# An LSTM on one core: VectorE's PSUM reads put ahead of the x sums, the cell over 128 columns, outer sums deferred

## The chip, the cores and the metric

The kernel runs on one core of one Trainium2 chip. Five engines of that core work side by side, each with its own queue that it takes strictly in order: TensorE (PE in the profile, its weight loads PEld), VectorE (DVE), ScalarE (ACT), GpSimd (POOL) and SyncE (SP), which here issues nearly all DMAs. [...] The metric is the time of one launch in microseconds (us), the median of several runs.

## The reference

An LSTM over 512 time steps, batch 32, input and state width 512, then a residual:

```python
xW = jnp.einsum('ntd,dg->ntg', x, Wx) + b          # x: 32 x 512 x 512, Wx: 512 x 2048
def step(carry, xw_t):
    prev_h, prev_c = carry
    a = xw_t + prev_h @ Wh                         # Wh: 512 x 2048
    i, f, o = sigmoid(a[:, :512]), sigmoid(a[:, 512:1024]), sigmoid(a[:, 1024:1536])
    g = jnp.tanh(a[:, 1536:])
    next_c = f * prev_c + i * g
    next_h = o * jnp.tanh(next_c)
out = x + hs                                       # hs: all next_h, h0 = cond_1024, c0 = 0
```

All of it is float32. `prev_h @ Wh` is a chain over the steps; `x @ Wx` depends on no step and can be made at any time before it is needed.

## The kernel before

**Layout.** A gate matrix of one time step (32 x 2048) is kept as 128 partitions (4 blocks of units x 32 batch rows) by 512 columns: two halves of 256, each four gates of 64 units. Two PSUM tiles `gates` take turns, one per step.

**The recurrence.** In step `k`, `h_part(k)` (L452) adds `h @ Wh` to `gates[k % 2]`, which `seed_gates` (ScalarE, L437) has filled with the step's x part from the SBUF tile `xw`. Then `cell(k)` runs: sigmoid, tanh, sigmoid on ScalarE (L482 to L484); on VectorE `f*c` (L486, 128 columns), and then by halves of 64 columns `i*g` (L491), `c` (L493), on ScalarE `tanh c` (L495), on VectorE `o*tanh c` (L498, written into the buffer called `fc`) and a transpose to `ht` (L507). `h_part(k+1)` reads `ht`. GpSimd adds `ht` to the residual x (L513, tile `oc`) and, for a later step, the bias to `xw` (L418).

**The x part.** `x @ Wx` is made in the gaps of the recurrence. Rows of 8 time steps go three at a time through a scheme of fast matrix multiplication with 20 products instead of 24 (lists `A_OPS`, `A_OF`, `B_OF`, `C_OPS`, `C_OF`), and each product through an inner scheme with 7 small products instead of 8. A superblock is 24 time steps (3 rows) and 20 products, which are called jobs. Windows are the slots for this work; from step 3 on there is one per step (`windows_of(k) = [k + 4]`). In a superblock's 24 windows the jobs start in five of every six (`begin`). One job spreads over six windows: in the window `v` of its start and the four behind it PE makes its small products 1, 5, 6, 7, 2, 3 and 4 (`products`, L273). Before them:

- x sums (VectorE): `node_sums` (L236) adds whole rows where the outer scheme wants it (128 x 512), and `inner_sums` (L203 to L206) makes the four 128 x 128 sums of a job. Both operands lie in SBUF. All are made in `prepare(v + 1)`, at the end of the window before the job's.
- `evacuate(v)` takes results out of PSUM: first `job.finish(half)` for the jobs that started five and four windows ago, which makes the outer sums (L380, VectorE, 128 x 512 a half, one operand in PSUM or both in SBUF; L371 is a plain ScalarE copy into a slot), and, with the second half, stores finished ones to DRAM (SP, L323). Then ScalarE copies `pu`, `p5`, `pp` (L297, L301, L307, L308) and VectorE adds `pu` (L304) and `pp` (L309), which read the PSUM tiles `acc`.

PE's first small product of a window is written into an `acc` tile, so it comes behind the VectorE and ScalarE reads of that tile.

**What sets the order.** The program is written in one order by hand (`tc.manual_schedule()`); each engine takes its own instructions in that order. Per step of the loop: `load_residual` and `load_xw(k+3)` (SP), `h_part(k)`, `seed_gates(k+1)`, `add_bias(k+2)`, then for the window `evacuate(v)`, `products(v)`, `fetch(v)` (SP: the factors `wa`, `wb` and, three windows ahead of a superblock, its three rows of x), `cell(k)`, and `prepare(v+1)`. So VectorE's queue between two cells reads: x sums of the next job, outer sums, `pu`, `pp`. While VectorE is in it, PE makes `h_part` and then the small products.

Jobs begin at step 10 (`START`, `LEAD = 22`): the steps before make three rows by another scheme and the 14 combined factors (`make_factors`). After the last job, from step 495 on, the gates are split in two halves of 64 units which overlap (`is_split`).

Of the kernel before, what the change touches and what calls it, by code (L numbers as in the profile page):

```python
# [1 line left out]

# [38 lines left out]
LEAD = 22  # L41
# [23 lines left out]
def kernel(  # L65
# [13 lines left out]
    npool = ctx.enter_context(tc.tile_pool(name="npool", bufs=7))  # L79
    spool = ctx.enter_context(tc.tile_pool(name="spool", bufs=6))  # L80
# [117 lines left out]
    def inner_sums(a, name):  # L198
# [3 lines left out]
        return s, [  # L202
# [13 lines left out]
    nodes = {}  # L216
# [7 lines left out]
    def node_sums(sb, n):  # L224

        ops = []

        def want(v):
            if v < 2 * MO or (sb, v) in nodes:
                return  # L230
            how, a, b = A_OPS[v - 2 * MO]
            want(a)
            want(b)
            dst = nodes[sb, v] = npool.tile([P, ROW, 2, B], F32, name=f"n_{sb}_{v}", tag="node")
            fn = nc.vector.tensor_add if how == "add" else nc.vector.tensor_sub
            ops.append(lambda: fn(dst, node(sb, a), node(sb, b)))  # L236

        want(A_OF[n])
        return ops

    def left(a, s, sums):
        if s in (1, 2, 4):
            return a(*{1: (0, 0), 2: (0, 1), 4: (1, 1)}[s])
        return sums[:, {5: 0, 6: 1, 7: 2, 3: 3}[s]]
# [37 lines left out]
    def products(v):  # L282
        for late, ss in ((1, (6,)), (4, (4,)), (2, (7,)), (0, (1,)), (0, (5,)), (1, (5,)), (3, (2, 3))):
            job = jobs.get(v - late)
            for s in ss if job else ():
                if s != 5 or job.w5 == v:
                    product(job, s)

    def evacuate(v):
        for half, late in ((1, 5), (0, 4)):  # L290
            job = jobs.get(v - late)
            if job:
                job.finish(half)
# [9 lines left out]
        if job:  # L303
            nc.vector.tensor_add(job.pu[:, 1], job.acc, job.p5)  # L304
        job = jobs.get(v - 3)
        if job:
            nc.scalar.copy(job.pp[0], job.pu)  # L307
            nc.scalar.copy(job.pp[1][:, 0], job.acc)  # L308
            nc.vector.tensor_add(job.pp[1][:, 1], job.acc, job.p5)  # L309

# [3 lines left out]
    spare = [const.tile([P, 2, 2 * C], F32, name=f"slot_{i}") for i in range(3)]  # L314
# [10 lines left out]
    def finish_unit(job, i, j):  # L325
        def finish(half):
# [3 lines left out]
            if half:  # L330
                store(i, j, job.f)
                free.append(job.f)

# [15 lines left out]
    for v in C_OF:  # L349
        uses[v] += 1  # L350
        if v < R:
            copied.add(v)
    sums, left_uses = {}, {}

    def finish_product(job, sb, n):
        def slot(v, half):
            if half == 0:
                sums[sb, v] = free.pop(0)
                left_uses[sb, v] = uses[v]
            return sums[sb, v][:, half]  # L360

        def done(v, half):
            if half and (sb, v) in left_uses:
                left_uses[sb, v] -= 1
                if left_uses[sb, v] == 0:
                    free.append(sums.pop((sb, v)))

        def finish(half):
            pp = job.pp[half].rearrange("p n c -> p (n c)")
            if n in copied:  # L370
                nc.scalar.copy(slot(n, half), pp)  # L371
# [3 lines left out]

            for v in by_ready[n]:
                how, a, b = C_OPS[v - R]
                fn = nc.vector.tensor_add if how == "add" else nc.vector.tensor_sub
                srcs = source(a), source(b)
                fn(slot(v, half), *srcs)  # L380
                for u in (a, b):
                    if u != n or n in copied:
                        done(u, half)
            for at, v in enumerate(C_OF):
                if ready[v] == n and half:
                    i, j = divmod(at, NJ)
                    store(HEAD // ROW + MO * sb + i, j, sums[sb, v])
                    done(v, half)
# [52 lines left out]
    HALVES = [slice(0, H), slice(H, P)]  # L441
# [23 lines left out]
    def cell(t):  # L465
# [9 lines left out]
        for part in [(0,), (1,)] if two else [(0, 1)]:  # L475
            units = slice(H * part[0], H * (part[-1] + 1))
            i = slice(part[0], part[-1] + 1)
            if two:
                g = half_of(t, part[0]).rearrange("p (h g u) -> p h g u", h=1, g=G)
            else:  # L480
                g = gates[t % 2].rearrange("p h (g u) -> p h g u", g=G)
            nc.scalar.activation(s[:, i, 0:2], g[:, :, 0:2], AF.Sigmoid)  # L482
# [210 lines left out]
```

## Time and profile before

| | |
|---|---|
| median of 3 runs (lowest, highest) | 3450.46 us (3447.96, 3450.6) |
| the profiled execution: its own time, its span | 3446.5 us, 3444.4 us |
| PE busy | 3170.1 us (92%) |
| VectorE busy | 2858.1 us (83%), 8502 instructions |
| ScalarE busy | 1529.9 us (44%) |
| GpSimd busy | 960.3 us (28%) |
| DMA | 649.90 MB, 189 GB/s on average |
| granted PE clock | 0.996 |

How to read the lines that follow. In a timeline each row has the start, the busy time, the engine, the line of the kernel, the operation, the tile written and those read with their shape, and how many instructions in a row it stands for; brackets at the end give how long the engine had been idle before and what released it. `x2` with 0.35 us means that two instructions of a group took that long together, since a second one starts before the first has ended. In a group row the two numbers behind the bar are the busy time in all (us) and the mean of one (ns), and behind the next bar idle time before it. In the view of waits a row has the total, the number and the longest, in us. In the view of stretches a row has the length and then, per engine, the busy time and the instructions in parentheses.

A step is counted from one L482 (the first sigmoid, which starts as soon as `h_part` has ended and ScalarE is free) to the next.

### The profile page before, as it was taken

Reading aid. Unit: us, or ns where it says so; the run is one execution under the profiler, and the core shown is the slowest. Engines: PE = TensorE matmul, PEld = TensorE weight load, DVE = VectorE, ACT = ScalarE, POOL = GpSimd, SP = SyncE. Lnnn points to the kernel's source line nnn. Section 1 sums busy time; section 2 is a strip of 40 time slices with the busy share of each in tenths; the row PEclk is TensorE's granted clock in tenths of the full one; section 3 lists DMA queues with packets and bytes.
Section 4 is the critical chain, followed back from the end, with each engine's and each line's share of the span. In section 5 each row is a group of like instructions: output and inputs, shape, how many; then the busy total and the mean of one; then the engine's idle time right before and its main releaser. Section 6 shows DMA issues by size and latency. Waiting matters only on the chain.

```text
span 3444.4 us, 103490 instructions
## 1 busy us (share of the span) xinstructions
PE 3170.1 (92%) x40948; PEld 1295.2 (38%) x40948; DVE 2858.1 (83%) x8502; ACT 1529.9 (44%) x4972; POOL 960.3 (28%) x1003
## 2 busy tenths in 40 slices
PE   8899999999999999999999999999999999999987
PEld 2433333333333333333333333333333333333334
DVE  5778888888888888988888888888888888888875
ACT  1344444444444444444444444444444444444433
POOL 0122322232222223222222222222223222232321
PEclk9999999999999999999999999999999999999999
DMA  4556665656666566656566565656565666666552
GB/s 179 168 192 211 187 211 177 209 175 198 190 190 215 169 212 195 202 168 215 173 203 190 189 209 178 211 185 210 167 216 170 205 190 187 208 184 214 173 154 66
DMA packets 324919, 649.90 MB, mean 189 GB/s; under 512 B 43600, under 2 KB 109264, under 8 KB 323920
## 3 DMA queue, kind: packets, MB, share of 16 engines
q1 hardware_dynamic: 324288, 643.28, 59.8%
q8 instruction: 320, 5.24, 0.7%
q14 instruction: 167, 1.37, 0.1%
q10 hardware_dynamic: 144, 0.01, 0.0%
HBM read 464.59 MB, written 178.52 MB: 187 GB/s over the span
## 4 chain that ended last, share of the span: by engine, by line
DVE 45%; PE 37%; ACT 6%; issue 6%; DMA 5%; POOL 1%; SPq 1%; DVEq 0%; POOLq 0%; ACTq 0%
PE gates L452 20%; PE acc L273 7%; DVE s L204 7%; PE pp L273 7%; DVE slot L380 4%; DVE n L236 4%; DMA row<-in_x_dram 4%; DVE s L203 3%; DVE pp L309 3%; DVE ht L507 3%; DVE s L205 3%; DVE raw L380 3%; DVE t L380 2%; DVE fc L498 2%; DVE ig L491 2%
## 5 line engine op out<-in xcount | busy, mean ns | idle before, releaser
L452 PE MATMUL gates<-wh_sb,ht 128*32 128x512 f32 (+1 forms) x16320 | 1820.0, 587 | 21.0 <-DVE fc L490 15.3
L513 POOL TENSOR_TENSOR oc<-xr,ht 128x128 f32<-128x128 f32 x495 | 304.2, 615 | 2406.6 <-DVE ht L507 1196.0
L452 PEld LDWEIGHTS gates<-wh_sb,ht 128*32 128x32 f32 x16320 | 521.6, 110 | 1033.0 <-issue 819.2
L418 POOL TENSOR_TENSOR xw<-xw,bias_sb 128x512 f32<-128x512 f32 x504 | 675.6, 1341 | 63.3 <-DMA xw<-xw 54.6
L482 ACT ACTIVATE s<-gates 128x256 f32<-128x256 f32 (+1 forms) x511 | 195.3, 382 | 695.0 <-PE gates L452 694.4
L307 ACT COPY pp<-pu 128x512 f32<-128x512 f32 x412 | 246.1, 597 | 368.6 <-DVE slot L380 166.8
L486 DVE TENSOR_TENSOR fc<-s,c 128x128 f32<-128x128 f32 x494 | 141.7, 287 | 271.6 <-ACT s L482 270.5
L495 ACT ACTIVATE ig<-c 128x64 f32<-128x64 f32 x1024 | 207.9, 248 | 288.8 <-DVE c L493 288.8
L273 PE MATMUL acc<-wa,s 128*32 128x256 f32 x2240 | 176.5, 387 | 160.3 <-DVE pp L309 157.7
L204 DVE TENSOR_TENSOR s<-s,n 128x128 f32<-128x128 f32 x280 | 288.4, 1030 | 9.7
L308 ACT COPY pp<-acc 128x256 f32<-128x256 f32 x412 | 146.9, 357 | 332.6 <-DVE slot L380 126.1
L437 ACT COPY gates<-xw 128x512 f32<-128x512 f32 x493 | 284.8, 578 | 20.0 <-DVE xw L410 19.7
L498 DVE TENSOR_TENSOR fc<-s,ig 128x64 f32<-128x64 f32 x1024 | 192.5, 226 | 103.4 <-ACT ig L495 103.4
L309 DVE TENSOR_TENSOR pp<-acc,p 128x256 f32<-128x256 f32 x412 | 175.5, 426 | 89.5 <-ACT pp L308 80.5
L273 PE MATMUL pp<-wb,n 128*32 128x256 f32 x3200 | 245.9, 379 | 0.0
L273 PEld LDWEIGHTS acc<-wa,s 128*32 128x32 f32 x2240 | 54.5, 108 | 382.9 <-DVE pp L309 322.4
L273 PE MATMUL acc<-wb,s 128*32 128x256 f32 x2240 | 172.6, 380 | 19.2 <-DVE pu L304 19.2
L491 DVE TENSOR_TENSOR ig<-s 128x64 f32<-128x64 f32 x1024 | 187.3, 223 | 0.0
L507 DVE STREAM_TRANSPOSE ht<-fc 128x64 f32<-128x64 f32 x990 | 184.1, 224 | 1.8 <-DVE fc L498 1.6
L493 DVE TENSOR_TENSOR c<-fc,ig 128x64 f32<-128x64 f32 x1024 | 182.9, 218 | 1.2
L297 ACT COPY pu<-acc 128x256 f32<-128x256 f32 x412 | 152.4, 370 | 50.7 <-PE acc L273 41.5
L273 PE MATMUL acc<-t,s 128*32 128x256 f32 x1920 | 146.3, 384 | 30.3 <-DVE pu L304 16.5
(140 smaller groups left out, 4290.1 us busy)
## 6 DMA issues: line engine op xcount, KB each, us to landing
wb<-keep_b SPq DMA_DIRECT2D x280, 512.0 KB, 5.1
xw<-xw SPq DMA_DIRECT2D x504, 256.0 KB, 4.0
wa<-keep_a SPq DMA_DIRECT2D x280, 384.0 KB, 4.2
xw<-slot SPq DMA_DIRECT2D x528, 128.0 KB, 2.3
xr<-in_x_dram SPq DMA_DIRECT2D x256, 128.0 KB, 3.2
out_dram<-oc SPq DMA_DIRECT2D x255, 128.0 KB, 2.5
row<-in_x_dram SPq DMA_DIRECT2D x63, 512.0 KB, 7.1
xw<-t SPq DMA_DIRECT2D x240, 128.0 KB, 2.3
```

The costliest lines, as they stand in the source:

```text
L204: lambda: v.tensor_sub(s[:, 1], s[:, 0], a(0, 0)),
L273: nc.tensor.matmul(dst[t * B : (t + 1) * B], a[:, t], w, start=s in (1, 5) and m == 0, stop=True, skip_group_check=True,)
L307: nc.scalar.copy(job.pp[0], job.pu)
L309: nc.vector.tensor_add(job.pp[1][:, 1], job.acc, job.p5)
L380: fn(slot(v, half), *srcs)
L418: nc.gpsimd.tensor_add(xw[t], xw[t], bias_sb)
L437: nc.scalar.copy(gates[t % 2], xw[t])
L452: nc.tensor.matmul(g[j * B : (j + 1) * B], state["ht"][:, k, :], wh_sb[:, k, j, cols], start=False, stop=True, skip_group_check=True,)
L491: nc.vector.tensor_mul(ig[:, u], s[:, i, 0], s[:, i, 3])
L498: nc.vector.tensor_mul(h[:, u], s[:, i, 2], tc_t[:, u])
L507: nc.vector.transpose(ht[:, 2 * i : 2 * i + 2].rearrange("p q b -> p (q b)"), h[:, HALVES[i]])
L513: (nc.gpsimd if not two else nc.vector).tensor_add(state["oc"][:, tt % 2], xr[t][:, tt % 2], ht)
```

## The change

Six things change. Nothing of the arithmetic does, but for the order of some additions being cut into other pieces.

1. **VectorE's order between two cells.** x sums are no longer made in `prepare`. `announce(v)` puts the sums of jobs up to three windows ahead (`AHEAD`) into a list `due`, each with the window in which it is wanted; `run_due` is called in the window behind `evacuate`, makes all that is wanted in this window, and fills up with others as long as the columns of the window (each instruction counted as its columns plus 160) stay under `ROOM = 3400`. The four inner sums of a job have their own tiles and windows (`s0` in the job's window, `s1` one later, and so on). Sums of rows take their tiles from a fixed set of 8.
2. **Outer sums deferred.** An outer sum whose operands are all in SBUF and whose result is wanted later is made as one 128 x 1024 instruction (L505) from the list, with a limit (`limit`, `SLACK`); its store is issued there. A call `run_due(v - 0.5, 0)` ahead of `evacuate`'s other work makes those that have reached their limit. The rest stay halves in `finish` (L489). There are four spare slots instead of three.
3. **The cell over 128 columns.** `i*g`, `c`, `tanh c`, `o*tanh c` and the transpose are one instruction each instead of two.
4. **Seeds.** `seed_gates(k + 2)` stands at the end of step `k`; before, `seed_gates(k + 1)` stood in step `k` behind `h_part`.
5. **Row loads** are issued six windows ahead of a superblock instead of three, in the order first, third, second.
6. **`LEAD` is 23 instead of 22**, so all jobs run one step earlier and the split steps begin one step earlier; the combined factors are made over five steps by two and then by one.

Its core (`before`, `after`):

```diff
-LEAD = 22
+LEAD = 23
+NODES = 8
+FIXED = 160
+ROOM = 3400
+SLACK = [1, 1, 3]
+AHEAD = 3
...
+    def push(window, columns, fn, ready):
+        insort(due, (window, next(order), columns, fn, ready))
+
+    def run_due(v, room):
+        i = 0
+        while i < len(due):
+            window, _, columns, fn, ready = due[i]
+            if window > v and (columns + FIXED > room or not ready(v)):
+                i += 1
+                continue
+            assert ready(window)
+            due.pop(i)
+            fn()
+            room -= columns + FIXED
+            i = 0
...
+        s = job.sums = [None] * 4
+        def push_sum(i, fn):
+            def go():
+                s[i] = spool.tile([P, 4, B], F32, name=f"s{i}_{sb}_{n}", tag=f"s{i}", bufs=(4, 6, 4, 4)[i])
+                fn(nc.vector, block(node(sb, A_OF[n])))
+            push(
+                job.w + i,
+                P,
+                go,
+                lambda v: v + 1 >= job.w + i
+                and (A_OF[n] < 2 * MO or (sb, A_OF[n]) in nodes)
+                and (i % 2 == 0 or s[i // 2] is not None),
+            )
...
     def evacuate(v):
+        run_due(v - 0.5, 0)
+        taken = 0
         for half, late in ((1, 5), (0, 4)):
             job = jobs.get(v - late)
             if job:
-                job.finish(half)
+                taken += job.finish(half)
...
             for v in by_ready[n]:
+                if v in at_half:
+                    put_out(sb, v)
+                    continue
+                def go(v=v):
+                    _, a, b = C_OPS[v - R]
+                    slot(sb, v)
+                    add(v)(sums[sb, v], sums[sb, a], sums[sb, b])
+                    used(sb, a)
+                    used(sb, b)
+                    put_out(sb, v)
+                push(START + PER * sb + limit[v] - 0.5, 8 * P, go, ...)
...
-            if not two:
-                nc.vector.tensor_mul(by_half(fc), s[:, :, 1], by_half(state["c"]))
-            for i in part:
...
-                nc.vector.tensor_mul(ig[:, u], s[:, i, 0], s[:, i, 3])
-            for i in part:
-                nc.vector.tensor_add(c[:, HALVES[i]], fc[:, HALVES[i]], ig[:, HALVES[i]])
-            for i in part:
-                nc.scalar.activation(tc_t[:, HALVES[i]], c[:, HALVES[i]], AF.Tanh)
...
+            nc.vector.tensor_mul(by_half(fc[:, u]), s[:, part, 1], by_half(state["c"][:, u]))
+            nc.vector.tensor_mul(by_half(ig[:, u]), s[:, part, 0], s[:, part, 3])
+            nc.vector.tensor_add(c[:, u], fc[:, u], ig[:, u])
+            nc.scalar.activation(tc_t[:, u], c[:, u], AF.Tanh)
+            nc.vector.tensor_mul(by_half(h[:, u]), s[:, part, 2], by_half(tc_t[:, u]))
...
+            nc.vector.transpose(ht[:, 2 * part.start : 2 * part.stop].rearrange("p q b -> p (q b)"), h[:, u])
...
-        sb, rest = divmod(v + 3 - START, PER)
-        if rest in (0, 1, 2) and 0 <= sb < NSB:
-            load_row(HEAD // ROW + MO * sb + rest)
+        sb, rest = divmod(v + 6 - START, PER)
+        if rest < MO and 0 <= sb < NSB:
+            load_row(HEAD // ROW + MO * sb + (0, 2, 1)[rest])
...
             h_part(k)
-            if 1 <= k < T - 1:
-                seed_gates(k + 1)
...
-                evacuate(v)
+                announce(v)
+                taken = evacuate(v)
+                run_due(v, ROOM - taken)
                 products(v)
...
+                if m == 0 and k + 2 < T:
+                    seed_gates(k + 2)
```

224 lines of the change are left out of this document (139 added, 85 removed).

## The prediction

> **What bounds the kernel now.** I read the page's span first, then the stretch in which all jobs run, then the view of waits, and last one step in the timeline.
>
> ```profile
> span 3444.4 us, 103490 instructions
> ```
> ```profile
> 182.53:3326.99 3144.46, 2932.26 (x37768) 1184.76 (x37764) 2682.68 (x7975) 1440.51 (x4642) 920.86 (x960) 1.00 0.62 193
> ```
> ```profile
> PEld acc L273 <- DVE pp L309: 422.5, 285, 4.8
> ```
>
> The stretch from the first sigmoid of step 10 to that of step 490 holds 480 steps, twenty superblocks: 3144.46 us, 157.2 us per 24 steps, 6.55 us a step. PE is busy for 2932 of the 3144 us, VectorE for 2683. The third row names what PE waits for: the weight loads of the small products stood 422 us for VectorE's `pp` add, the last instruction VectorE makes before a cell. One step shows why it is late:
>
> ```profile
> 1727.77 0.38 ACT L482 ACTIVATE s<-gates 128x256 f32<-128x256 f32 x1 [3.92 <-PE gates L452]
> ...
> 1728.19 0.29 DVE L486 TENSOR_TENSOR fc<-s,c 128x128 f32<-128x128 f32 x1 [0.72 <-ACT s L482]
> ...
> 1728.40 0.35 DVE L491 TENSOR_TENSOR ig<-s 128x64 f32<-128x64 f32 x2
> ...
> 1728.67 0.35 DVE L493 TENSOR_TENSOR c<-fc,ig 128x64 f32<-128x64 f32 x2
> ...
> 1728.92 0.40 ACT L495 ACTIVATE ig<-c 128x64 f32<-128x64 f32 x2 [0.42 <-DVE c L493]
> ...
> 1729.21 0.37 DVE L498 TENSOR_TENSOR fc<-s,ig 128x64 f32<-128x64 f32 x2 [0.18 <-ACT ig L495]
> ...
> 1729.54 0.37 DVE L507 STREAM_TRANSPOSE ht<-fc 128x64 f32<-128x64 f32 x2
> 1729.74 0.36 ACT L297 COPY pu<-acc 128x256 f32<-128x256 f32 x1
> ...
> 1729.84 3.64 PE L452 MATMUL gates<-wh_sb,ht 128*32 128x512 f32 x32
> ...
> 1730.04 0.46 POOL L513 TENSOR_TENSOR oc<-xr,ht 128x128 f32<-128x128 f32 x1 [5.18 <-issue]
> 1730.12 0.53 DVE L204 TENSOR_TENSOR s<-s,row 128x128 f32<-128x128 f32 x1
> 1730.27 0.60 ACT L307 COPY pp<-pu 128x512 f32<-128x512 f32 x1
> ...
> 1730.46 1.32 POOL L418 TENSOR_TENSOR xw<-xw,bias_sb 128x512 f32<-128x512 f32 x1
> 1730.57 1.36 DVE L205 TENSOR_TENSOR s<-row 128x128 f32<-128x128 f32 x1
> ...
> 1730.79 0.35 ACT L308 COPY pp<-acc 128x256 f32<-128x256 f32 x1
> ...
> 1731.86 0.28 DVE L206 TENSOR_TENSOR s<-row,s 128x128 f32<-128x128 f32 x1
> ...
> 1732.06 0.67 DVE L380 TENSOR_TENSOR raw<-t,pp 128x512 f32<-128x512 f32 x1
> ...
> 1732.77 0.69 DVE L380 TENSOR_TENSOR slot<-slot,raw 128x512 f32<-128x512 f32 x1
> ...
> 1733.48 2.13 SPq L323 DMA_DIRECT2D xw<-slot  x4
> 1733.54 0.38 ACT L482 ACTIVATE s<-gates 128x256 f32<-128x256 f32 x1 [2.40 <-PE gates L452]
> 1733.71 0.42 DVE L309 TENSOR_TENSOR pp<-acc,p 128x256 f32<-128x256 f32 x1
> ...
> 1734.04 0.28 DVE L486 TENSOR_TENSOR fc<-s,c 128x128 f32<-128x128 f32 x1
> ...
> 1734.18 0.64 PE L273 MATMUL acc<-wa,s 128*32 128x256 f32 x8 [0.71 <-DVE pp L309]
> ```
>
> Seen from the end of the transposes (L507, 1729.91): VectorE begins with the x sums. GpSimd begins at 1730.04 too, and holds until 1731.78 (0.46 + 1.32). In that time a sum with both operands in SBUF does not get through: L204 takes 0.53 and L205 1.36 us, ending with GpSimd's instruction, where L206 right behind takes 0.28. The outer sum with a PSUM operand comes at 1732.06, the `pp` add at 1733.71, 3.8 us after the transposes. PE ended `h_part` at about 1733.5, waited 0.71 us, and the next cell's first multiply (L486) had to queue behind the add as well. How much a group loses is seen in its mean:
>
> ```profile
> L204 DVE TENSOR_TENSOR s<-s,n 128x128 f32<-128x128 f32 x280 | 288.4, 1030 | 9.7
> ```
>
> At 0.28 us a piece these 280 would have taken 78 us, not 288.
>
> Two other steps give the floors. PE needs this much for `h_part` and six small products, without a wait between:
>
> ```profile
> 1703.64 3.62 PE L452 MATMUL gates<-wh_sb,ht 128*32 128x512 f32 x32
> ...
> 1709.66 0.61 PE L452 MATMUL gates<-wh_sb,ht 128*32 128x512 f32 x4
> ```
>
> That is 6.02 us a step. And the step quoted above has the shortest distance between two sigmoids, 1727.77 to 1733.54, 5.77 us: the cell (2.07 us to PE's start) and `h_part` alone. So the jobs' steps now take 6.55 us, where PE asks for 6.02 in the five of six windows with six products, and the recurrence for 5.77 in the sixth, with five.
>
> **The change part by part.**
>
> *VectorE's order.* Between two cells VectorE now makes outer halves (start to start 0.61 us, as 1732.77 to the next add), `pu` and `pp` (0.34 each, 1733.71 to 1734.04), then x sums (0.20 each, 1731.86 to 1732.06) and sums of rows (512 columns, 0.61). GpSimd's two instructions still take 1.8 us from the transposes on, but beside PSUM reads: the outer sum of 1732.06 needs 0.67 us, and I take that for beside GpSimd too, the nearest row. If it were blocked as the x sums are, the order would bring nothing; that end goes to the range.
>
> The new bound on the `pp` add is ScalarE: it copies `pu`, `p5`, `pp`, `pp` (1729.74 to 1731.14, 1.4 us in all, up to 1.7 if none overlaps), and VectorE's add waits for the last. That wait exists already:
>
> ```profile
> DVE pp L309 <- ACT pp L308: 80.5, 105, 7.8
> ```
>
> It now comes each step at 1.6 to 1.7 us behind the transposes, 2.1 to 2.2 in the steps with a copy into a slot (512 columns, 0.60 as L307). A usual step: one outer half and `pu`, 0.95; wait to 1.7; `pp` to 2.05; four sums to 2.85; one sum of rows to 3.45. VectorE is due at the next L486: PE starts 0.08 behind the transpose (1729.84 against the first half's end, 1729.76), the sigmoid 3.70 behind that (1733.54), L486 0.42 behind the sigmoid, 4.2 us in all. PE's first product is due at 3.7. Both are met. I added up all 24 windows in this way by the changed program's order of instructions. Most end between 2.6 and 3.8. Two with a deferred sum ahead and two with `pp` at 2.2 and six instructions behind end just at 4.1 to 4.2; I take 0.3 us for the four. One has two sums of rows behind `pp` and ends at 4.5: 0.3. One has three outer sums, one of them from SBUF and held until GpSimd's end at 1.9, so that `pp` ends at 4.0 to 4.2 and PE's products start 0.5 late. Together 1.1 us per 24 steps.
>
> *Deferred sums.* 280 halves from SBUF become 140 of 1024 columns: by starts 1.14 instead of 2 x 0.61 us, 0.08 x 140 = 11 us of VectorE time, all beside PE and counted above. Where one stands first it holds off GpSimd's `oc` for 1.1 us, and with it SP's store of `oc`, the loads of `xr` and `xw` and the stores of the outer sum queued behind. Those four stores are then issued until about 5.1 us behind the transposes (1.7 for L505 and `oc`, some 1.3 for three issues, 2.1 for the four as at 1733.48) and landed at 7.4:
>
> ```profile
> xw<-slot SPq DMA_DIRECT2D x528, 128.0 KB, 2.3
> ```
>
> In two windows VectorE writes the slot again in the next step, at 6.06 + 1.8 = 7.9. I take nothing for it; if it is late by half a us in each, it costs 20 us. `xw` is loaded a whole step ahead of its use on GpSimd, and stays so.
>
> *The cell.* VectorE's and ScalarE's instructions on the chain go from 64 to 128 columns, and no second half runs beside the first:
>
> ```profile
> L491 DVE TENSOR_TENSOR ig<-s 128x64 f32<-128x64 f32 x1024 | 187.3, 223 | 0.0
> L507 DVE STREAM_TRANSPOSE ht<-fc 128x64 f32<-128x64 f32 x990 | 184.1, 224 | 1.8 <-DVE fc L498 1.6
> ...
> L486 DVE TENSOR_TENSOR fc<-s,c 128x128 f32<-128x128 f32 x494 | 141.7, 287 | 271.6 <-ACT s L482 270.5
> ...
> L463 DVE STREAM_TRANSPOSE x_last<-xr 128x128 f32<-128x128 f32 x1 | 0.3, 305 | 0.0
> ```
>
> 128 columns take 0.064 us more than 64 (287 against 223 ns); that falls on `i*g`, `c`, `tanh c` and the last multiply, 0.26, and 0.08 on the transpose (305 against 224), which PE awaits whole now. `c` started 0.27 us behind `i*g`, 0.05 more than one half takes, and that gap goes: 0.29 in all. The recurrence needs 5.77 + 0.29 = 6.06 us, just above PE's 6.02. So all 24 windows take 6.06, and the recurrence takes over from PE. Bounds: nothing (PE stays the limit, 6.02) to 0.4.
>
> [...]
>
> *Seeds.* `gates<-xw` was, and is, ScalarE's first instruction behind a cell's `tanh c`. The queue keeps its order; nothing.
>
> *Row loads.*
>
> ```profile
> DVE n L236 <- DMA row<-in_x_dram: 14.6, 13, 4.1
> ```
>
> Thirteen superblocks waited here for the last row, which held up everything behind it on VectorE. Six windows ahead, the wait goes; the buffers used are free by then, so SP isn't held. Its worth is inside 6.55 to 6.06.
>
> *LEAD.* One step of the head is replaced by a split step of the tail:
>
> ```profile
> 169.94 0.39 ACT L482 ACTIVATE s<-gates 128x256 f32<-128x256 f32 x1 [2.08 <-PE gates L452]
> ...
> 182.53 0.38 ACT L482 ACTIVATE s<-gates 128x256 f32<-128x256 f32 x1 [2.08 <-PE gates L452]
> 3434.40 0.28 ACT L482 ACTIVATE s<-gates 128x128 f32<-128x128 f32 x1 [1.21 <-PE gates L452]
> ...
> 3438.80 0.28 ACT L482 ACTIVATE s<-pp 128x128 f32<-128x128 f32 x1 [1.78 <-PE pp L452]
> ```
>
> The head's last step takes 12.6 us; a split step takes 4.4. I take it (an estimate) that half of the 12.6 is factor making that moves into earlier steps: -2 us, between +4 (all of it moves) and -8 (none).
>
> *Sum.* Jobs' steps: 480 x 6.06 + 20 x 1.1 = 2931 against 3144, -213; LEAD -2: -215. The profiled execution takes 3446.5 us (2.1 around the span); the median shown is 3450.46, 4 us (0.1%) above it. 3450 - 215 = 3235 us.
>
> **The rivals.**
>
> *PE's floor.* The merged cell isn't longer and nothing slips: 480 x 6.02 = 2890, -254, and -2: 3194 us. For it: the spacing of two halves (0.35) is little less than one of 128. Against: the transposes, which PE awaited by halves.
>
> *ScalarE takes the place of the x sums.* If VectorE stands at `pp` later than I add up, because ScalarE's copies queue for the tiles that VectorE's outer sums still read, every cell starts some 0.3 us late: 480 x 6.36 = 3053, -91, and -2: 3357 us. For it: the row of 105 waits. Against: the copies took 1.4 us in the quoted step, where nothing held them. [...]
>
> *Slower: the store queue.* SP takes its DMAs in order. A deferred sum's stores wait there for an instruction that ends up to 3 us behind the transposes, and four issues take 2.1 us (1733.48); the next step's `xw` load stands behind them, and behind that GpSimd's bias, the seed and `h_part`. With no slack in `xw`, 140 deferred sums cost 2.1 us each, 294, more than the 215 won: 3529 us. It decides from 215 / 140 = 1.5 us each. Against: in the quoted step the four issues follow an outer sum that ends later, 3.5 us behind the transposes, and `h_part` did not wait.
>
> *Nothing moves.* The wait is for a tile, not for the time of the add; then order is no lever, and the merged cell hides in PE's waits: 3450 us. Against: the first product started 0.05 us behind the add's end.
>
> **How the numbers follow.** My forecast 0.58, PE's floor 0.17, ScalarE's place 0.15, slower 0.08, nothing moves 0.02. The predicted time is 3235 us. The range goes from 3190 (PE's floor and 4 us for the head) to 3360 (ScalarE's place): the first two cases alone would be 0.75, with the third it is 0.90. Within 0.2% of 3450 us, about what a measurement of this kernel tells from no change, lies only the last: faster 0.90, same 0.02, slower 0.08.
>
> **What would show each step.** In the changed profile: the four x sums near 0.28 us, where L204 and L205 had 1.03 and up; PE's waits for `pp` down from 422 us to under 100; VectorE's busy time down by at least 500 us (210 from L204, 0.6 x 494 from the cell). The distance from `f*c` to PE's start up from 1.65 to about 1.94 us. Steps even at 6.0 to 6.1 us. No wait for rows. The prediction is wrong where outer sums from PSUM take over 0.7 us beside GpSimd, where the `pp` add ends later than 3.6 us behind the transposes in most steps, or where outer sums wait for DMAs.

## The result, and the profile after

The changed kernel takes 3272.45 us (median; 3271.71 to 3273.69), against 3450.53 us (3447.96 to 3454.49) for the kernel before on the same chip: a ratio of 0.9483, with a 95% interval from 0.9467 to 0.9500. It is 178 us faster; the forecast was 3235 us in a range from 3190 to 3360, so 215 us were promised and 178 came. The profiled execution took 3272.1 us.

From the page of the changed kernel, the span, VectorE's share among the busy times, and the chain that ended last by engine:

```profile
span 3270.2 us, 101636 instructions
PE 3163.7 (97%) x40980; PEld 1297.2 (40%) x40980; DVE 2290.2 (70%) x6388; ACT 1473.4 (45%) x4482; POOL 931.3 (28%) x1002
...
PE 75%; DVE 12%; issue 5%; ACT 5%; DMA 1%; POOL 1%; SPq 0%; DVEq 0%; ACTq 0%; POOLq 0%
```

The stretch of the jobs' 480 steps, now from the first sigmoid of step 9 to that of step 489 (length, then busy time per engine):

```profile
187.60:3151.25 2963.65, 2925.81 (x37832) 1193.14 (x37828) 2114.33 (x5908) 1387.07 (x4165) 891.67 (x960) 1.00 0.64 205
```

The view of waits of the changed kernel (total, number, longest):

```profile
PEld gates L579 <- DVE ht L620: 222.6, 469, 1.7
...
DVE pp L383 <- ACT pp L382: 176.9, 205, 8.0
...
PEld acc L342 <- DVE pp L383: 53.0, 38, 7.3
...
PE acc L342 <- DVE pp L383: 21.3, 5, 6.4
...
DVE slot L489 <- DMA xw<-slot: 5.8, 7, 1.4
```

And two of its groups on VectorE, an x sum (the counterpart of the old L204) and the transpose:

```profile
L306 DVE TENSOR_TENSOR s<-s,node 128x128 f32<-128x128 f32 x280 | 80.4, 287 | 0.0
...
L620 DVE STREAM_TRANSPOSE ht<-fc 128x128 f32<-128x128 f32 (+1 forms) x528 | 162.3, 307 | 56.9 <-DVE fc L615 3.7
```

The jobs' steps went from 3144.46 to 2963.65 us, 6.17 a step. PE's wait for `pp` fell from 422 to 53 us; the wait on PE's list that replaced it is the one for `ht`, the end of the cell. VectorE lost 568 us of busy time in these steps (at least 500 were forecast, 0.6 a step of them from the cell: by the rows of the prediction 2 x 223 - 287 ns for each of `i*g`, `c` and the last multiply, and 2 x 224 - 305 for the transpose), and the sum that took 1030 ns takes 287. One step of the changed kernel:

```profile
1719.68 0.38 ACT L608 ACTIVATE s<-gates 128x256 f32<-128x256 f32 x1 [2.35 <-PE gates L579]
...
1720.10 0.29 DVE L611 TENSOR_TENSOR fc<-s,c 128x128 f32<-128x128 f32 x1 [0.70 <-ACT s L608]
...
1720.31 0.28 DVE L612 TENSOR_TENSOR ig<-s 128x128 f32<-128x128 f32 x1
1720.62 0.29 DVE L613 TENSOR_TENSOR c<-fc,ig 128x128 f32<-128x128 f32 x1
...
1721.01 0.31 ACT L614 ACTIVATE ig<-c 128x128 f32<-128x128 f32 x1 [0.61 <-DVE c L613]
...
1721.35 0.29 DVE L615 TENSOR_TENSOR fc<-s,ig 128x128 f32<-128x128 f32 x1 [0.43 <-ACT ig L614]
...
1721.74 0.31 DVE L620 STREAM_TRANSPOSE ht<-fc 128x128 f32<-128x128 f32 x1
1721.98 0.39 DVE L377 TENSOR_TENSOR pu<-acc,p 128x256 f32<-128x256 f32 x1
1722.11 3.64 PE L579 MATMUL gates<-wh_sb,ht 128*32 128x512 f32 x32 [0.34 <-DVE ht L620]
...
1722.55 1.28 POOL L546 TENSOR_TENSOR xw<-xw,bias_sb 128x512 f32<-128x512 f32 x1
...
1723.66 0.43 DVE L383 TENSOR_TENSOR pp<-acc,p 128x256 f32<-128x256 f32 x1 [1.29 <-ACT pp L382]
1724.00 0.28 DVE L305 TENSOR_TENSOR s<-node 128x128 f32<-128x128 f32 x1
...
1725.82 0.38 ACT L608 ACTIVATE s<-gates 128x256 f32<-128x256 f32 x1 [2.20 <-PE gates L579]
```

VectorE's `pp` add stands at 1723.66, waits for ScalarE's copy as forecast, and ends 2.04 us behind the transpose (1722.05). The x sums follow when GpSimd is through (1722.55 + 1.28 = 1723.83) and take 0.28 us each. VectorE has time to spare: at the next sigmoid (1725.82) it is waiting. What sets this step, 6.14 us, is the cell: from `f*c` (1720.10) to PE's start (1722.11) it takes 2.01 us, where it took 1.65 before.

### The profile page after: what moved, and what is told of

Same layout as the page of the kernel before. It is cut to its first block, busy times and chain, and to the rows that moved or that the text cites. A ratio compares the mean times of both kernels' runs of the same rounds, so it can differ in the third digit from the quotient of the medians.

```text
span 3270.2 us, 101636 instructions
## 1 busy us (share of the span) xinstructions
PE 3163.7 (97%) x40980; PEld 1297.2 (40%) x40980; DVE 2290.2 (70%) x6388; ACT 1473.4 (45%) x4482; POOL 931.3 (28%) x1002
## 4 chain that ended last, share of the span: by engine, by line
PE 75%; DVE 12%; issue 5%; ACT 5%; DMA 1%; POOL 1%; SPq 0%; DVEq 0%; ACTq 0%; POOLq 0%
PE gates L579 46%; PE pp L342 12%; PE acc L342 11%; PE p L342 4%; ACT s L608 2%; ACT ig L614 2%; DVE fc L611 2%; DVE ht L620 1%; DVE fc L615 1%; DVE c L613 1%; DVE ig L612 1%; POOL xw L546 1%; DVE wb_make L191 1%; DMA xw<-slot 1%; PE pp L579 1%
## 5 line engine op out<-in xcount | busy, mean ns | idle before, releaser
L611 DVE TENSOR_TENSOR fc<-s,c 128x128 f32<-128x128 f32 (+1 forms) x529 | 155.7, 294 | 400.4 <-ACT s L608 396.6
L614 ACT ACTIVATE ig<-c 128x128 f32<-128x128 f32 (+1 forms) x530 | 162.0, 306 | 337.5 <-DVE c L613 337.5
L383 DVE TENSOR_TENSOR pp<-acc,p 128x256 f32<-128x256 f32 x412 | 177.7, 431 | 191.7 <-ACT pp L382 176.9
L615 DVE TENSOR_TENSOR fc<-s,ig 128x128 f32<-128x128 f32 (+1 forms) x530 | 153.3, 289 | 221.6 <-ACT ig L614 221.6
L342 PE MATMUL pp<-wb,node 128*32 128x256 f32 x3200 | 247.0, 379 | 0.0
L620 DVE STREAM_TRANSPOSE ht<-fc 128x128 f32<-128x128 f32 (+1 forms) x528 | 162.3, 307 | 56.9 <-DVE fc L615 3.7
L377 DVE TENSOR_TENSOR pu<-acc,p 128x256 f32<-128x256 f32 x412 | 168.8, 410 | 15.9 <-ACT p L374 11.8
L342 PE MATMUL pp<-wb,s 128*32 128x256 f32 x2240 | 172.7, 379 | 0.0
L342 PE MATMUL p<-wa,s 128*32 128x256 f32 x2240 | 172.7, 379 | 0.0
L613 DVE TENSOR_TENSOR c<-fc,ig 128x128 f32<-128x128 f32 (+1 forms) x530 | 152.3, 287 | 18.4
L374 ACT COPY p<-p 128x256 f32<-128x256 f32 x412 | 154.7, 375 | 5.1 <-PE p L342 5.1
```

The source lines that it names most:

```text
L342: nc.tensor.matmul(dst[t * B : (t + 1) * B], a[:, t], w, start=s in (1, 5) and m == 0, stop=True, skip_group_check=True,)
L611: nc.vector.tensor_mul(by_half(fc[:, u]), s[:, part, 1], by_half(state["c"][:, u]))
L613: nc.vector.tensor_add(c[:, u], fc[:, u], ig[:, u])
L614: nc.scalar.activation(tc_t[:, u], c[:, u], AF.Tanh)
L615: nc.vector.tensor_mul(by_half(h[:, u]), s[:, part, 2], by_half(tc_t[:, u]))
L620: nc.vector.transpose(ht[:, 2 * part.start : 2 * part.stop].rearrange("p q b -> p (q b)"), h[:, u])
```

## The experiments

Each ratio is to the kernel before, on the same chip. "Steps" are the 480 job steps in the profiled execution, from first sigmoid to first sigmoid.

| kernel | median, us | ratio (95% interval) | steps, us |
|---|---|---|---|
| before | 3450.53 | 1 | 3144.5 |
| changed | 3272.45 | 0.9483 (0.9467 to 0.9500) | 2963.7 |
| before, order alone | 3260.44 | 0.9456 (0.9443 to 0.9470) | 2956.9 |
| before, no bias add on GpSimd | 3241.27 | 0.9406 (0.9389 to 0.9423) | 2953.2 |
| before, cell over 128 alone | 3522.32 | 1.0220 (1.0198 to 1.0241) | 3216.2 |
| changed, sums first | 3469.77 | 1.0055 (1.0039 to 1.0072) | 3159.0 |
| changed, cell in halves | 3190.52 | 0.9252 (0.9240 to 0.9265) | 2885.1 |
| changed, last two links in halves, old seeds | 3218.77 | 0.9334 (0.9314 to 0.9354) | 2919.8 |
| changed, old seeds | 3261.56 | 0.9459 (0.9446 to 0.9472) | 2961.4 |
| **halves and old seeds** | **3183.78** | **0.9229 (0.9215 to 0.9242)** | 2885.6 |
| the same, no deferral | 3271.85 | 0.9482 (0.9468 to 0.9496) | 2968.4 |
| the same, no deferral, no bias add | 3183.88 | 0.9230 (0.9214 to 0.9246) | 2898.7 |
| the same (with deferral), LEAD 22 | 3192.12 | 0.9251 (0.9238 to 0.9265) | 2889.2 |
| the same (with deferral), LEAD 24 | 3188.12 | 0.9243 (0.9227 to 0.9260) | 2895.7 |

**The order alone.** In the kernel before, the job's sums move from the end of the window before to behind `evacuate`:

```diff
                 evacuate(v)
+                if v >= START:
+                    for op in prepare(v):
+                        op()
                 products(v)
...
-                for op in prepare(v + 1):
-                    op()
+                if v + 1 < START:
+                    for op in prepare(v + 1):
+                        op()
```

> The kernel before with one thing changed: the x sums of a job are made behind evacuate in the window of the job instead of at the end of the window before; no deferral, no spreading, cell in halves, old seeds and loads. Theory (the order itself carries the gain): PE's wait for pp falls from 422 to under 120 us, the step from 6.55 to 6.1 to 6.2, the time 3230 to 3300 us. Rival (the gain needs the sums to be spread over windows and the outer sums deferred, since windows with several sums of rows run over): 3350 us or more.

Measured: 3260.44 us. Its stretch:

```profile
186.39:3143.24 2956.85, 2899.52 (x37768) 1200.38 (x37764) 2382.79 (x7974) 1430.46 (x4642) 819.29 (x960) 1.00 0.64 206
```

So the order, with nothing else, takes 188 us from the jobs' steps, all of the change's 181. By the starts of its sigmoids 18 of 24 steps stand at 6.02 to 6.07 or 5.77 us; five are 0.3 to 0.55 us longer and one, the last of a superblock, takes 7.7. PE's wait for `pp` fell to 158 us, not under 120.

**GpSimd's bias add left out.** The kernel before, x sums still first:

```diff
-                add_bias(k + 2)
+                pass
```

> The kernel before without GpSimd's bias add to xw, so the bias is left out of the gates of most steps; all else as before, the x sums still first. Theory (the x sums came late because VectorE could not read SBUF beside GpSimd's 1.3 us add): the mean of L204 falls from 1.03 to under 0.4 us, L205 likewise, pp comes 1 to 1.3 us sooner, and the time falls to 3250 to 3320 us with the old order. Rival (the order and the amount of work count, not GpSimd): the time stays above 3400 us.

Measured: 3241.27 us. Its stretch, and one group:

```profile
178.61:3131.77 2953.16, 2906.82 (x37768) 1200.45 (x37764) 2240.63 (x7975) 1434.29 (x4642) 294.40 (x480) 1.00 0.65 206
```
```profile
L204 DVE TENSOR_TENSOR s<-s,n 128x128 f32<-128x128 f32 x280 | 90.2, 322 | 9.7
```

This kernel leaves the bias out of most steps' gates. With the old order, one GpSimd instruction less per step takes 191 us from the steps, as much as the order did, and L204 falls from 1030 to 322 ns. So the order matters because of what GpSimd does at that time: the two remedies are for the same cost.

**The x sums first again.** The changed kernel with one call moved:

```diff
-                taken = evacuate(v)
-                run_due(v, ROOM - taken)
+                run_due(v, ROOM - 1800)
+                evacuate(v)
```

> The changed kernel with one call moved: the x sums that are due, and the deferred outer sums, ahead of evacuate instead of behind it; spreading, cell and seeds as changed. Theory (the place in VectorE's queue counts, because GpSimd holds the first SBUF sums until 1.8 us behind the transposes): L204's kind of sum is back above 0.8 us, the pp add ends 1.3 us or more later, the step goes from 6.17 to 6.4 to 6.55, the time 3380 to 3450 us. Rival (spreading the sums over windows and deferring carry the gain, the place does not): 3270 to 3320 us.

The call that moves also makes the deferred outer sums, so these go ahead too.

Measured: 3469.77 us, 19 us (0.55%, interval 0.39% to 0.72%) slower than the kernel before, and 20 us above what I expected. From its timeline, and its waits:

```profile
1718.28 0.31 DVE L620 STREAM_TRANSPOSE ht<-fc 128x128 f32<-128x128 f32 x1
...
1719.25 1.33 POOL L546 TENSOR_TENSOR xw<-xw,bias_sb 128x512 f32<-128x512 f32 x1
1719.36 1.37 DVE L308 TENSOR_TENSOR s<-node,s 128x128 f32<-128x128 f32 x1
...
1722.54 0.43 DVE L383 TENSOR_TENSOR pp<-acc,p 128x256 f32<-128x256 f32 x1
```
```profile
PEld acc L342 <- DVE pp L383: 452.3, 307, 7.3
```

The `pp` add ends 4.4 us behind the transpose (1718.59), and PE's wait for it is back. Without the order, all the rest of the change together brings nothing. The merged cell is a loss in that sum: against the kernel before with the merged cell alone (3216.2 us in the steps, below), the 3159.0 here leave some 57 us for spreading, deferral and the row loads.

**The cell in halves.** The changed kernel, the four VectorE links and `tanh c` per half of 64 columns as before:

```diff
+            hs = [u] if two else [slice(0, H), slice(H, P)]
-            nc.vector.tensor_mul(by_half(ig[:, u]), s[:, part, 0], s[:, part, 3])
+            for e in hs:
+                nc.vector.tensor_mul(ig[:, e], s[:, e.start // H, 0], s[:, e.start // H, 3])
...
```

> The changed kernel with i*g, c, tanh c, o*tanh c and the transpose in halves of 64 columns as before. Theory (the cell over 128 columns sets the step): from f*c to PE's start goes from 1.96 to 2.01 us back to about 1.65, the recurrence to 5.77 to 5.85, and PE sets the step: 6.02 to 6.05 in the 20 windows with six products, 5.8 in the other four, some 144.5 us per 24 steps instead of 148.1, the time 3195 to 3225 us. Rival (PE or VectorE's order sets the 6.08 to 6.14 already): 3265 to 3285, the merged cell costs nothing.

Measured: 3190.52 us, 82 less than the changed kernel (80 by the ratios). Its stretch, and the first sigmoids of three steps, between them one with five products and one with six:

```profile
187.10:3072.24 2885.14, 2884.14 (x37832) 1228.64 (x37828) 2183.00 (x7828) 1430.13 (x4646) 891.46 (x960) 1.00 0.65 210
```
```profile
1715.23 0.38 ACT L608 ACTIVATE s<-gates 128x256 f32<-128x256 f32 x1 [2.90 <-PE gates L579]
...
1721.00 0.38 ACT L608 ACTIVATE s<-gates 128x256 f32<-128x256 f32 x1 [2.40 <-PE gates L579]
...
1727.02 0.38 ACT L608 ACTIVATE s<-gates 128x256 f32<-128x256 f32 x1 [2.35 <-PE gates L579]
```

PE is busy for 2884.14 of 2885.14 us. The six-product steps take 6.02 us, the five-product steps 5.77, as the prediction's two floors said; a superblock takes 144.3 us against 148.2. VectorE is 69 us busier than in the changed kernel, and it costs nothing.

**The last two links alone in halves.** The changed kernel with the old seeds; `i*g`, `c` and `tanh c` stay at 128 columns:

```diff
-            nc.vector.tensor_mul(by_half(h[:, u]), s[:, part, 2], by_half(tc_t[:, u]))
+            for e in hs:
+                nc.vector.tensor_mul(h[:, e], s[:, e.start // H, 2], tc_t[:, e])
...
-            nc.vector.transpose(ht[:, 2 * part.start : 2 * part.stop] ..., h[:, u])
+            for e in hs:
+                nc.vector.transpose(ht[:, 2 * (e.start // H) : 2 * (e.start // H) + 2] ..., h[:, e])
```

> The changed kernel with the old seeds, and of the cell only o*tanh c and the transpose in halves; i*g, c and tanh c stay at 128 columns. Theory (links add up: from o*tanh c to PE's start 0.63 us in halves against 0.76 whole, so the recurrence is 5.95 to 6.01 instead of 6.08 to 6.14): PE sets the 20 windows with six products at 6.02, the other four take 5.95 to 6.01, 144.9 us per 24 steps, 3190 to 3210 us. Rival (PE waits for the whole of ht, or half instructions cost as much on the chain as whole ones): steps at 6.08 or more, 3240 us and above.

Measured: 3218.77 us, between the two theories. The links did add up: the five-product steps, which show the recurrence, take 6.01 us, the six-product steps 6.02. What the sum lacked are three steps per superblock in which VectorE or the products are late (6.34, 6.38 and 6.49 us; 6.10, 6.21 and 6.25 with all of the cell in halves): 0.65 us more per 24 steps, 13 in all.

**The cell over 128 columns alone**, in the kernel before:

```diff
-            for i in part:
-                u = HALVES[i]
...
-                nc.vector.tensor_mul(ig[:, u], s[:, i, 0], s[:, i, 3])
+            nc.vector.tensor_mul(by_half(ig[:, u]), s[:, i, 0], s[:, i, 3])
...
```

> The kernel before with one thing changed: i*g, c, tanh c, o*tanh c and the transpose over 128 columns. Theory (the cell is a chain of dependent links in every step, also where VectorE's queue sets the step, since VectorE idles between the links): each step is 0.25 to 0.4 us longer, the time 3560 to 3640 us. Rival (where VectorE is the bound, five instructions fewer per step give it time back, or the longer cell hides in PE's 422 us of waits): 3400 to 3455 us.

Measured: 3522.32 us, 77 above the 3445.72 of the kernel before in that comparison. Its sign is the theory's, its size half of it. The five-product steps at the recurrence's floor went from 5.77 to 6.14 us, but of the others ten grew by 0.18 to 0.36, two by less than 0.1, and eight of 24, all of 6.7 us and more in the kernel before, not at all or got shorter. Why those did not grow, no run here separates. VectorE's busy time in the jobs' steps fell by 68 us, and the kernel got 2.2% slower.

**Deferral.** The changed kernel with the cell in halves and the old seeds (its own run is told further below), and without deferral; every outer sum stays two halves in `finish`:

```diff
+    at_half = set(range(R, len(ready)))
     sums, left_uses = {}, {}
```

> The changed kernel with the cell in halves and the old seeds, and beside these no outer sum deferred: all are made as halves in finish, ahead of pu and pp. Theory (a half whose operands both lie in SBUF stands right behind the transposes, where GpSimd holds it to 1.72 us instead of 0.68, as in the run with the order alone, where five windows of 24 were 0.3 to 0.55 us over PE's step and one 1.6): 1.5 to 3.5 us more per 24 steps, 3210 to 3250 us. Rival (deferral saves 11 us of VectorE time, which is hidden): 3175 to 3187.

Measured: 3271.85 us, 88 more than with deferral, twice the middle of what I expected. The last step of a superblock takes 8.1 us instead of 6.25:

```profile
1805.88 0.65 DVE L490 TENSOR_TENSOR slot<-pp,slot 128x512 f32<-128x512 f32 x1
...
1806.50 1.28 POOL L547 TENSOR_TENSOR xw<-xw,bias_sb 128x512 f32<-128x512 f32 x1
1806.56 1.77 DVE L490 TENSOR_TENSOR slot<-slot,raw 128x512 f32<-128x512 f32 x1
...
1808.26 0.68 DVE L490 TENSOR_TENSOR slot<-slot,t 128x512 f32<-128x512 f32 x1
1808.86 0.68 DVE L490 TENSOR_TENSOR t<-pp,slot 128x512 f32<-128x512 f32 x1
...
1809.96 0.43 DVE L383 TENSOR_TENSOR pp<-acc,p 128x256 f32<-128x256 f32 x1
```

The half with a PSUM operand (`pp`, a tile that PE's products were written to) takes 0.65 us, the next, with both operands in SBUF, 1.77 beside GpSimd, the one behind GpSimd's end 0.68.

**No deferral and no bias add.** The same kernel with the bias add left out as above.

> The changed kernel with the cell in halves, the old seeds and no outer sum deferred, and without GpSimd's bias add to xw, so the bias is left out of the gates of most steps. Theory (what deferral saved is mostly GpSimd's hold on SBUF halves that stand right behind the transposes, 1.77 us instead of 0.68): of the 4.1 us per 24 steps some 2 to 3.5 go, 3200 to 3235 us. Rival (it is the number of outer sums ahead of pu and pp alone): 3260 to 3275 us.

Measured: 3183.88 us, the same total as with deferral and the bias add, but not by the steps alone. Of the 83 us that the lack of deferral cost in the steps, 70 are gone with the GpSimd instruction and 13 stay: the last step of a superblock still takes 7.04 us, against 6.25 with deferral. The total comes out even because head and tail, which lose the bias add too, are some 15 us shorter than with deferral (3.6 of them ahead of the first sigmoid). One group of SBUF halves, without deferral and then without deferral and bias add:

```profile
L490 DVE TENSOR_TENSOR slot<-slot,t 128x512 f32<-128x512 f32 x42 | 50.8, 1210 | 1.2
```
```profile
L490 DVE TENSOR_TENSOR slot<-slot,t 128x512 f32<-128x512 f32 x42 | 29.0, 691 | 1.2
```

**The old seeds.**

```diff
             h_part(k)
+            if 1 <= k < T - 1:
+                seed_gates(k + 1)
...
-                if m == 0 and k + 2 < T:
-                    seed_gates(k + 2)
```

> The changed kernel with the seeds put back: seed_gates(k + 1) behind h_part. Theory (ScalarE's queue): in steps 0 to 2 the seed stands ahead of ScalarE's copies of the later window and waits 13.1 us for VectorE's xw add, so PE idles 9.8 us for pu. With the seeds back the first three steps take 22.6 to 24 us again instead of 24.5, 26.4 and 26.9, the time falls by 6 to 8 us to about 3265, and the jobs' steps stay as they are. Rival (the clock): the head lost its time because the first steps ran at a lower granted clock; then the time stays within 2 us of 3272.

Measured: 3261.56 us. The intervals of this ratio and of the changed kernel's touch (0.9472 and 0.9467), so the traces decide. Step 0 in the changed kernel:

```profile
54.48 0.68 DVE L538 TENSOR_TENSOR xw<-gates,bias_sb 128x512 f32<-128x512 f32 x1
...
55.25 0.59 ACT L565 COPY gates<-xw 128x512 f32<-128x512 f32 x1 [13.13 <-DVE xw L538]
55.78 0.37 ACT L370 COPY pu<-acc 128x256 f32<-128x256 f32 x1
...
56.20 2.36 PE L342 MATMUL acc<-t,s_h 128*32 128x256 f32 x20 [9.76 <-ACT pu L370]
```

The same with the old seeds:

```profile
39.35 0.37 ACT L370 COPY pu<-acc 128x256 f32<-128x256 f32 x1
40.21 0.37 ACT L374 COPY p<-p 128x256 f32<-128x256 f32 x1 [0.49 <-PE p L342]
43.40 1.05 PE L342 MATMUL acc<-t,s_h 128*32 128x256 f32 x16
...
52.39 0.59 ACT L565 COPY gates<-xw 128x512 f32<-128x512 f32 x1 [11.80 <-DVE xw L538]
```

ScalarE's seed waits for VectorE's `xw` add in both. In the changed kernel the copies of the step's second window stand behind it, in step order, and PE's next products wait for them; with the old seeds `pu` is copied at 39.35 and the products start at 43.40. The first three steps take 22.76, 23.90 and 23.72 us with the old seeds, 24.45, 26.41 and 26.92 with the new ones, 7.4 us in all. In these steps the granted clock was 0.85 in the three profiles with the new seeds and 0.88 to 0.90 in the eleven with the old; how much of the 7.4 us is the wait itself and how much the lower clock, no run separates. The jobs' steps are the same to 2.3 of 2963.7 us.

**Halves and old seeds together.**

> The changed kernel with both parts put back: the cell in halves and the seeds behind h_part. Theory (the two costs lie in different stretches, steps against head, so they add): 3190.5 - 10.9 = 3179.6 us, between 3175 and 3184. Rival (they overlap: with shorter steps the head's wait was hidden anyway): 3188 to 3192.

Measured: 3183.78 us, the fastest kernel here. By the ratios the seeds bring 8 us on top of the halves (the intervals touch, 0.9242 and 0.9240), against 7.4 in the first steps above and 8.7 in those of these two traces: the two costs lie in different stretches and add. The 3179.6 worked out for the sum was 4 us low; the 10.9 us it used for the seeds is more than any of these.

**LEAD 22 and 24**, with halves and old seeds (at 24, two factors in each of the first six steps):

```diff
-LEAD = 23
+LEAD = 22
```

> The changed kernel with the cell in halves and the old seeds, and LEAD 22 instead of 23. Theory (by the trace with the old seeds, whose way from the first sigmoid to the first job's step is 140.0 us against 145.0, and whose tail is 2.7 us longer than before): 2 to 3 us more than with LEAD 23, about 3182. Rival (the factors only move; worth nothing, or the other sign): 3174 to 3180.

> The changed kernel with the cell in halves and the old seeds, LEAD 24 instead of 23, and two factors made in each of the first six steps. Theory (a head step of 7 to 12 us is replaced by a split step of 4 to 5, as between LEAD 22 and 23, where it brought 8 us): 3 to 8 us less than 3184. Rival (the factors that have to be made a step sooner lengthen the steps before by as much): 3182 to 3190.

Measured: 3192.12 and 3188.12 us, against 3183.78 with 23. Both missed what I expected: with 22 I had 2 to 3 us more, and with 24 3 to 8 us less. From 22 to 23 the ratio falls from 0.9251 to 0.9229, 8 us (the intervals overlap by 0.0004): in the traces the way from the first sigmoid to the first job step falls by 7.2 us, and the jobs' steps by 3.5. From 23 to 24 that way shortens by another 5.7 us, but the jobs' steps get 10.1 us longer; the intervals overlap, so there is no gain to be told.

## Why the prediction came out as it did

Against the sum (jobs' steps 2931, head and tail 2 us less than before), the profile shows 2963.65 and 6.6 us more (head 187.60 against 182.53, tail 118.95 against 117.41): 32.6 and 8.6 us, less the 4 us by which the profiled execution before lay under its median. That is the 37 us between 3235 and 3272.

- *VectorE's order*: right in mechanism; the prediction has no price for it alone. Alone it gives 188 us, where the whole change gives 181; leaving the bias add out gives 191; undoing the order gives all of it back. The `pp` add ends where the tally put it, at 2.04 against 2.05 us. Outer sums from PSUM take 0.65 to 0.69 us, beside GpSimd too (0.67 assumed). PE's wait for `pp` is 53 us by the row that had 422, under the 100.
- *The cell*: the term that failed. 0.29 us was too small; it is 0.31 in five of 24 steps and 0.37 in 19, so from `f*c` to PE 1.96 and 2.02 us where 1.94 was forecast. Link by link, from the step quoted in the prediction and the one above: `f*c` to `i*g` 0.21 and 0.21, to `c` 0.27 and 0.31, to `tanh c` 0.25 and 0.39, to the multiply 0.29 and 0.34, to the transpose 0.33 and 0.39, to PE 0.30 and 0.37. I let the 0.05 between `i*g` and `c` go as a gap between halves; it did not go. And I took 0.064 for `c`, by the duration of VectorE's instruction, where the start of `tanh c` behind it moved by 0.14. By medians over all superblocks it moved by 0.08 in the five steps and by 0.14 in the 19; the 0.06 more goes with a second semaphore instruction on ScalarE, told at the end. So steps without a slip take 6.08 or 6.14 us, not 6.06: some 1.7 us per 24 steps, 34 in all, which is the 32.6 that the steps missed by.
- The slips, 1.1 us per 24 steps, came out at 1.05, in part by luck. What was forecast is in place but smaller, 0.62 by medians: the step with two sums of rows is 0.31 us over (0.3 forecast), the one with three outer sums 0.23 (0.5), and the four windows put at 4.1 to 4.2 us cost 0.08 in one (0.3). The rest is single steps that I had not forecast, some 9 us in all, the longest two in the first superblock (1.6 and 1.2 us).
- *Deferred sums*: credited with 11 us of hidden VectorE time. Their worth is 88 us (83 in the steps), mostly because a half from SBUF right behind the transposes runs into GpSimd: 70 of the 83 go with the bias add. The total did not suffer, since the tally of the windows had the sums where the change puts them. The slots rewritten before their store had landed are there, 5.8 us in seven waits on `slot` and as much again on `t`. Their price is small: the four longest (1.2 to 1.4 us) are each followed by a step that is 0.36 to 0.64 us over, 2.2 us in all, against the 20 named for half a us in each.
- *Seeds*, "the queue keeps its order; nothing": wrong for the steps 0 to 2, right for the others. I looked at steps with one window; the first three have two, and at the end of the step the seed stands ahead of the second window's copies. 7 to 9 us.
- *LEAD*: -2 between +4 and -8. It was -8 by the times, at the end of the range. That head and tail are 6.6 us longer all the same has three places: 3.05 us ahead of the first sigmoid (40.54 against 37.49 us), where the granted clock was lower in this execution, told at the end; 2.0 from there to the first job step, where the seeds take back what LEAD gave; 1.5 in the tail.
- *Row loads*: no wait for rows is left, as forecast; with the order alone only one is left too (4.0 us). Taken together, spreading and early rows show no gain of their own: without deferral the steps take 2968 us, with the order alone 2957.

The rivals: *PE's floor* did not come, and what kept it away is the merged cell alone, with halves it comes at 3190.5 us, for which the prediction had 3194. *ScalarE takes the place*: VectorE's waits for ScalarE's copies doubled, from 80.5 to 176.9 us. They are 197.4 us with the cell in halves, and there PE is busy for 2884.14 of 2885.14 us, so they hold up next to nothing. *The store queue*: a store lands 3.3 us after its issue instead of 2.3, and GpSimd's bias add does wait for DMAs more than before, in the jobs' steps 27 times and 30 us in all (16 of them and 14.8 us in the row below), against three times and 1.0 us. But nearly all of it is slack: the slips that the prediction did not forecast are some 9 us together, so this can hardly have cost more, where the rival had 294. *Nothing moves*: refuted by the order alone. The row is from the waits of the changed kernel in the jobs' stretch:

```profile
POOL xw L546 <- DMA xw<-xw: 14.8, 16, 2.8
```

So in the jobs' steps: about -188 from the order, about -71 from the rest of the sums' handling (deferral -83, the rest +12), +78 from the merged cell.

By VectorE's busy time the merged cell is the cheaper one (2114 us in the steps against 2183 with halves), and the time went the other way, by 82 us after the change and by 77 in the kernel before. In this chain of dependent links the second half ran beside the next link, and a whole instruction does not: `tanh c` starts 0.25 us behind `c` in the step of the kernel before and 0.39 in that of the changed one.

## What to carry to other kernels

Before counting what an engine does, look at which of its instructions are held up by another engine, and when: here one GpSimd instruction of 1.3 us per step decided where VectorE's SBUF sums could stand. In the kernel before, the order and the removal of that instruction were two ways to the same 190 us; with the order in place, deferral and the removal were two ways to most of the 83 that halves from SBUF cost. On a chain that sets the step, price each link by the distance between starts, not by an instruction's duration, and keep halves that overlap even where they cost busy time (here 69 us of it, and the launch was 82 us shorter). When a line moves past a loop, check the first iterations, which have more in them than the ones that were looked at.

## What the runs showed that I had not expected

- The hold is whole, and it goes both ways. From 1500 to 2100 us, 87 VectorE sums from SBUF start during GpSimd's bias add in the kernel before and 41 in the changed one, and each ends 0.14 us or more behind it; the one at 1806.56 above takes 1.77 us and ends 0.55 behind the add, where the next takes 0.68 in all. The group of SBUF halves of 512 columns shown above takes 691 ns on average without the bias add and 1210 with it, a PSUM half 0.65 to 0.69 us in either case; and GpSimd's `oc`, 0.46 us as a rule, takes 1.34 beside a 1024-column sum, as two rows of the run with the sums first show:

```profile
1724.76 1.18 DVE L505 TENSOR_TENSOR slot<-slot,slot 128x1024 f32<-128x1024 f32 x1
1724.92 1.34 POOL L626 TENSOR_TENSOR oc<-xr,ht 128x128 f32<-128x128 f32 x1 [4.34 <-DVE ht L620]
```

- The first `h_part` ran at about 0.62 of its speed in some executions:

```profile
34.57 5.84 PE L579 MATMUL gates<-wh_sb,h_init 128*32 128x512 f32 x32
```

  In the changed kernel it took 5.84 us, with the old seeds, where nothing before it differs, 3.62. In the fourteen profiled executions the first sigmoid stands at 37.4 to 37.8 us in seven and at 40.0 to 41.4 in seven, the same program parts ahead of it. The clock granted to PE separates them: from 35 to 37 us it was 0.50 in each of the late seven and 1.00 in each of the early seven. The stretch in the changed kernel, and then with the old seeds (length, busy time per engine, granted clock third from the end):

```profile
35.00:37.00 2.00, 2.00 (x12) 0.39 (x8) 1.90 (x5) 0.23 (x1) 0.00 (x0) 0.50 0.03 8
```
```profile
35.00:37.00 2.00, 2.00 (x24) 0.57 (x20) 1.90 (x5) 0.00 (x0) 0.00 (x0) 1.00 0.00 0
```

  Why the clock fell that early in some executions is open. A head is compared from the first sigmoid on.
- `tanh c` starts 0.39 us behind `c` in 19 of 24 steps of a superblock and 0.33 in the other five. In the trace of the changed kernel ScalarE has a separate semaphore instruction ahead of `tanh c` in 378 of the 480 job steps, and there the distance is 0.38 us or more; in the 102 without one it is 0.32 to 0.33:

```profile
L614 ACTq EVENT_SEMAPHORE  x402: 17/17/17, 66.3 to 3266.8; - x134
```

  The kernel before and the one with the cell in halves have no such instruction at this place. 378 times 0.06 us are some 23 of the 78 us that the merged cell costs (an estimate). What brings the second wait in, no run here shows.
